# Early-fusion transformer on one core: the last three runs' sums are cut in two, and the first part's order is made with other durations

## Chip, cores and metric

One core of a Trainium2 chip. The metric is device time in microseconds (us) of one execution; lower is better.

The engines named here: PE (TensorE: matrix products and transposes), DVE (VectorE), ACT (ScalarE), POOL (GpSimd) and SP (SyncE, which here only issues DMAs). Each engine works through a queue of its own in the order in which the program was built; ACT and POOL issue DMAs too. An instruction waits in its queue until the semaphores it names have come, and everything behind it waits with it.

## The reference, cut to what matters

Sixteen samples. A tokenizer (a 2x2 convolution and attention over 441 image tokens) and 128 text tokens give 569 rows of 256 numbers per sample. Layer 0 is attention in windows of 64 rows and then a mixture of 8 experts, of which each row takes its best two. Layer 1 is a linear attention by phases and then an LSTM over the 569 rows, whose output goes through running sums:

```python
h = tokenizer(x); h = concatenate([h, txt], axis=1)            # (16, 569, 256)
h = h + window_attention(layernorm(h))                         # layer 0
h = h + top2_of_8_experts(layernorm(h))
h = h + phase_attention(layernorm(h))                          # layer 1
return h + lstm_ffn(layernorm(h))

def lstm_ffn(x):                                               # (b, t, d)
    lstm_out = lstm(x, W_ih, W_hh, b_ih, b_hh)
    logits = lstm_out @ W_lin.T + b_lin                        # (b, t, 2)
    g = argmax(logits, axis=-1)[..., None]                     # 0 or 1
    w = g * lstm_out
    inc = cumsum(w, axis=1)
    prefix = inc - w
    suffix = inc[:, -1:, :] - inc
    return 2.0 * lstm_out + prefix * fw_att + suffix * bw_att
```

`inc[:, -1:, :]` is the total over all 569 rows, and every row of the output needs it (`suffix`). No row can leave before the last step of the LSTM is done and its sum is known.

## The kernel before

**Orders made by a planner.** The class `Order` (L163) takes a number of streams, which are Python generators. A stream yields the engine and the time that its next piece of work is taken to need (`yield "DVE", 0.43`), or an event to wait for, and then issues the instruction. `Order.run` always lets the stream go on whose piece can start first, by its own account of when each engine comes free. `first.fork(...)` starts a further stream at that point. The yielded times thus only decide the order in which instructions stand in each queue; they are no times of the chip. `"64"` behind a time names the tile shape of the products, `DVE+` and `POOL+` name work of DVE and POOL that the planner does not let run at one time.

**First part (about 0 to 962 us of the span; `first`, an `Order`).** Samples go in 8 pairs `p`, each with 9 chunks `c` of 128 rows (`unit(n)` gives pair and chunk of the n-th of 72 units). The streams: `features` (the convolution, DVE and ACT), `projections` and two `tokens` streams (image attention, mostly PE), `norms` (layernorm ahead of the windows, slot `"w"`), four `windows` streams (each has one unit at a time: transposes, q and k products, scores `wS`, maximum `wtop`, the subtraction of the maximum on POOL at L794, exp on ACT, sums, transposes `wpt`, products `wav` and `wob`), `sent_rows` (layernorm ahead of the experts), `routing` (which two experts) and `send` (POOL issues an indirect DMA for each of a chunk's two copies, L927, into the experts' regions `XS`). `norm` (L657) is used by `norms` and `sent_rows`: statistics on DVE (L661, L664), then on POOL add EPS (L668) and power -1/2 (L669), and for the windows a third one, power +1/2, into the last column of `h` (L671); then DVE subtracts and multiplies (L673). The column is read much later, by L784, on DVE.

**Second part (962 to about 3261 us).** The expert tiles, then the phase attention and the LSTM, ordered by another `Order`, `plan`. The LSTM (`steps`) is a chain of 569 steps, one about every 2.5 us where it runs alone: `gates` products (L1832) on PE, `act` (L1853) on ACT, then on DVE `ab`, the cell, its transposition, `th` on ACT, and `X` (L1896) on DVE, which the next step's products read.

**The sums.** `RUNS` cuts the 569 rows into runs of at most 16 rows; the last three have 16, 8 and 1. For each run `sums_of` (a stream `all_sums`) works once the run's steps are done. What leads to the total: the products for the logits (L1116 `fin`, PE), the carry from the run before (L1926, ACT), `w` (L1931, DVE, twice), the running sum `sum` (L1939, DVE scan, twice). Then the run's rows: `y` (L1946 and L1951, DVE, four pieces), transposes `turned` (L1959, PE), and the addition of the rows kept from before into the tile `O` (L1968, DVE). `fin` and `turned` share one PSUM buffer (tag `fin`).

**The end.** `all_rows` (L2017, DVE) spreads the total, `last` (L2025, L2027, PE) turns it, into the same PSUM buffer; `T1` (L2029) is its copy, for all rows, with L2034 a second copy for the run of one row. Then DVE adds it to the rows in `O` in pieces of 2, 4 and 8 units (L2038; a unit is 128 rows x 256 numbers, 128 KB) and SP and ACT in turn issue the stores of each run (L2042), two units each.

The line numbers in the text are those of the kernel before.

Of the kernel before, what the change touches and what calls it, by code (L numbers as in the profile page):

```python
# [10 lines left out]
F32 = mybir.dt.float32  # L11
# [10 lines left out]
E = 8  # L22
# [275 lines left out]
def kernel(ctx: ExitStack, tc: tile.TileContext, a: dict, out: bass.AP):  # L298
# [301 lines left out]
    def tokens(slot):  # L600

        last = NIMG - 384
        for n in range(slot, 7 * NP, 2):
# [4 lines left out]
            for m in range(2):  # L608
                yield "PE", 0.76, "64"
                for s in range(2):  # L610
                    nc.tensor.matmul(
                        sc[64 * s : 64 * s + 64, :NIMG], QT[s][:, m, 64 * c : 64 * c + 64],
                        fTs[2 * p + s][:, m, :], start=(m == 0), stop=(m == 1),
                    )
# [20 lines left out]
            for t in range(4):  # L635
                m = min(128, NIMG - 128 * t)
                yield "PE", 0.44, "64"
                for s in range(2):
                    nc.tensor.matmul(
                        mm[64 * s : 64 * s + 64, :], PT[:m, t, 64 * s : 64 * s + 64],  # L640
                        TV[s][:m, t, :], start=(t == 0), stop=(t == 3),
                    )
# [14 lines left out]
    def norm(h, to, name, slot):  # L657

        st = wk.tile([128, 6], F32, name=f"{name}_st", tag=f"st{slot}", bufs=1)
        yield "DVE", 0.43  # L660
        nc.vector.bn_stats(st, h[:, :D])  # L661
        mv = wk.tile([128, 2], F32, name=f"{name}_mv", tag=f"mv{slot}", bufs=1)
        yield "DVE", 0.18
        nc.vector.bn_aggr(mv, st)  # L664
        rstd = wk.tile([128, 1], F32, name=f"{name}_rstd", tag=f"rstd{slot}", bufs=1)
        yield "POOL", 0.85 if name[0] == "r" else 1.28
        over = mv[:, 1:2]
        nc.gpsimd.tensor_scalar(over, over, EPS, None, ALU.add)  # L668
        nc.gpsimd.tensor_tensor(rstd, over, mhalf[:, :1], ALU.pow)  # L669
        if name[0] == "w":  # L670
            nc.gpsimd.tensor_tensor(h[:, D + E :], over, half, ALU.pow)  # L671
        yield "DVE+", 0.5
        nc.vector.tensor_scalar(to, h[:, :D], mv[:, 0:1], rstd, ALU.subtract, ALU.mult)  # L673
        return rstd

    def norms():
# [10 lines left out]
    def sent_rows(p, c, h, slot):  # L687
# [9 lines left out]
        rstd = yield from norm(h, XN[p][:, c, :D], f"r{p}_{c}", slot)  # L697
        yield "DVE", 0.19
        nc.vector.scalar_tensor_tensor(
# [4 lines left out]
    def half_of_keys(u, kb, qk, rows, engine):  # L704
        for r in rows:
            own = slice(32 * r, 32 * r + 32)
            yield engine, 0.4
            (nc.scalar.copy if engine == "ACT" else nc.vector.tensor_copy)(
                kb[own, :, :, r, :], qk[own, 1].rearrange("p m (w x) -> p m w x", w=2)
            )  # L710
        first.mark(("keys", u, engine))

    def windows(slot):

        kb, vb = KB[slot], VB[slot]
        for n in range(slot, NC * NP, WINDOWS):
# [13 lines left out]
            for m in range(2):  # L730
                for j in range(2):
                    for k in range(2):
                        yield "PE", 0.25
                        nc.tensor.matmul(  # L734
                            qk[:, j, m, :], wqkv[:, k, D * j + 128 * m : D * j + 128 * m + 128],
                            xT[:, k, :], start=(k == 0), stop=(k == 1),
                        )
# [35 lines left out]
            for k in range(2):  # L773
                yield "PE", 0.06, "64"
                for w in range(2):
# [6 lines left out]
            nc.vector.tensor_reduce(top, S, AX.X, ALU.max)  # L782
# [968 lines left out]
    run_of = {(j, u): r for r, (j, u, _) in enumerate(RUNS)}  # L1751
    sums = {}

# [152 lines left out]
    def sums_of(r, j, u, n, X):  # L1906
# [14 lines left out]

        w = ls.tile([128, 2, NB, n + 1], F32, name=f"w{r}", tag="w2", bufs=1)
        yield "ACT", 0.2
# [5 lines left out]
        for k in range(2):  # L1929
# [4 lines left out]
            )  # L1934
        before = ls.tile([128, 2, NB, n + 1], F32, name=f"sum{r}", tag="sum", bufs=2)
        sums[r] = n, before
        for k in range(2):
# [27 lines left out]
        if "O" in tail:  # L1965
            o = tail["O"][:, tail["at"] : tail["at"] + units, :]
        for i in range(units):
# [4 lines left out]
        if "O" not in tail:  # L1972
            nc.sync.dma_start(PD[:, tail["at"] : tail["at"] + units, :], o)
            tail["stored"] += units
        tail["at"] += units

# [54 lines left out]
    for r, (j, u, n) in enumerate(RUNS):  # L2031
        units, t0 = -(-n // STEPS), BLOCKS[j][0] + u
        if n == 1:
            nc.vector.tensor_copy(by_q(T1[:NB]), last[:NB, 1].rearrange("p k (q x) -> p q k x", q=4))  # L2034
            nc.vector.tensor_tensor(O[:NB, at, :], O[:NB, at, :], T1[:NB], ALU.add)
        elif at == done:
# [3 lines left out]
                T1.unsqueeze(1).to_broadcast([128, done - at, D]), ALU.add,  # L2040
            )
        (nc.sync, nc.scalar)[r % 2].dma_start(  # L2042
            by_rows(out, t0, n),
# [124 lines left out]
```

## Time and profile before

| | |
|---|---|
| device time, median of 3 runs | 3315.19 us (3311.05 to 3320.17) |
| device time of the profiled execution | 3305.14 us |
| its span, first to last instruction | 3303.4 us |
| busy: PE / DVE / ACT / POOL | 2989.9 / 2051.8 / 1486.8 / 815.6 us |
| mean granted TensorE clock | 0.975 |
| first part up to the first expert tile's transposes | 0 to 961.95 us |
| last LSTM step's `X` ends | 3260.77 us |
| DMA queues 1 and 10 in the last 48 us | 4.74 and 4.59 MB |

A busy time is the sum of the times of an engine's instructions, so 2989.9 us of PE says that PE is at work in 91% of the span, in the mean over stages that are limited by different things. A row of the view by windows gives the same for one stretch of time: each engine's busy time with its number of instructions, the granted clock of TensorE, the share of time in which the 16 DMA engines were busy, and what they moved. In the timeline a row is an instruction or several merged: start, length, engine, line, operation, output and inputs, shape, how many, and in brackets how long the engine stood idle before it and what ended that.

### The profile page before, as it was taken

Reading aid. Unit: us, or ns where it says so; the run is one execution under the profiler, and the core shown is the slowest. Engines: PE = TensorE matmul, PEld = TensorE weight load, DVE = VectorE, ACT = ScalarE, POOL = GpSimd, SP = SyncE. Lnnn points to the kernel's source line nnn. Section 1 sums busy time; section 2 is a strip of 40 time slices with the busy share of each in tenths; the row PEclk is TensorE's granted clock in tenths of the full one; section 3 lists DMA queues with packets and bytes.
Section 4 is the critical chain, followed back from the end, with each engine's and each line's share of the span. In section 5 each row is a group of like instructions: output and inputs, shape, how many; then the busy total and the mean of one; then the engine's idle time right before and its main releaser. Section 6 shows DMA issues by size and latency. Waiting matters only on the chain.

```text
span 3303.4 us, 133968 instructions
## 1 busy us (share of the span) xinstructions
PE 2989.9 (91%) x57598; PEld 2205.3 (67%) x57598; DVE 2051.8 (62%) x6946; ACT 1486.8 (45%) x5068; POOL 815.6 (25%) x1579
## 2 busy tenths in 40 slices
PE   6999999999849999997899999999999999899884
PEld 3666666666638888885576767677676766666552
DVE  4678777786742222222676777677777777676555
ACT  3544544454412222222554556556665656454442
POOL 1354465545533332322311101010110010000000
PEclk8999999999979999998999999999999999999997
DMA  5111221101177676773433333333333333233323
GB/s 180 58 62 57 74 85 63 52 31 45 41 240 247 242 254 236 250 245 121 125 89 102 89 91 96 99 92 98 92 88 97 89 100 87 74 96 92 101 86 116
DMA packets 268419, 378.43 MB, mean 115 GB/s; under 512 B 133088, under 2 KB 207888, under 8 KB 255152
## 3 DMA queue, kind: packets, MB, share of 16 engines
q1 hardware_dynamic: 242192, 313.73, 30.1%
q0 software_dynamic: 14160, 38.83, 3.1%
q10 hardware_dynamic: 11472, 17.30, 1.8%
q8 instruction: 451, 7.39, 0.9%
q14 instruction: 144, 1.18, 0.1%
HBM read 252.06 MB, written 117.70 MB: 112 GB/s over the span
## 4 chain that ended last, share of the span: by engine, by line
PE 36%; DVE 7%; ACT 6%; DMA 2%; issue 2%; POOL 0%; SPq 0%; ACTq 0%; DVEq 0%; POOLq 0%
PE gates L1832 13%; PE xm_False L1116 6%; PE out_gate L1841 2%; PE v L1116 2%; ACT act L1853 1%; PE ek L1116 1%; PE eq L1116 1%; ACT th L1889 1%; DMA xo<-XOD 1%; PE r_False L1116 1%; DVE ab L1868 1%; PE po_False L1116 1%; DVE cT L1881 1%; PE ds_False L1116 1%; DVE act L1874 1%
## 5 line engine op out<-in xcount | busy, mean ns | idle before, releaser
L1832 PE MATMUL gates<-W_hh,X 128*16 128x96 f32 (+1 forms) x18176 | 490.8, 248 | 63.9 <-DVE X L1896 60.3
L1832 PEld LDWEIGHTS gates<-W_hh,X 128*16 128x16 f32 (+1 forms) x18176 | 378.3, 103 | 252.9 <-DVE X L1896 236.1
L1327 ACT ACTIVATE hT<-hp,w 128x256 f32<-128x256 f32 (+1 forms) x332 | 132.9, 453 | 448.8 <-PE hp L1320 342.0
L1853 ACT ACTIVATE act<-gates 128x96 f32<-128x96 f32 x568 | 142.1, 250 | 412.1 <-PE gates L1832 403.4
L1116 PE MATMUL xm_False<-W_ih,dxT_False 128*32 128x256 f32 x4352 | 294.3, 382 | 0.8 <-ACT dxT_False L1356 0.6
L1868 DVE SCALAR_TENSOR_TENSOR ab<-act 128x64 f32<-128x64 f32 x568 | 127.9, 225 | 255.6 <-ACT act L1853 248.5
L1334 PE MATMUL y<-w,hT 128*128 128x256 f32 x1208 | 276.3, 381 | 6.9 <-ACT hT L1327 6.8
L1340 DVE TENSOR_TENSOR ys<-y,w 128x512 f32<-128x512 f32 (+1 forms) x83 | 53.4, 644 | 358.5 <-PE y L1334 306.6
L1320 PE MATMUL hp<-xt,w 128*128 128x256 f32 (+1 forms) x1328 | 275.2, 360 | 0.0
L1775 PEld LDWEIGHTS <-nil 128*32 128x32 bf16 x4552 | 186.4, 95 | 119.0 <-issue 60.4
L1334 PEld LDWEIGHTS y<-w,hT 128*128 128x128 f32 x1208 | 226.3, 190 | 41.8 <-ACT hT L1327 11.8
L1320 PEld LDWEIGHTS hp<-xt,w 128*128 128x128 f32 x1328 | 232.8, 190 | 28.7 <-ACT hT L1327 0.2
L1261 POOL DMA_INDIRECT YT<-ys,to x151 | 147.3, 975 | 416.8 <-DVE ys L1340 389.6
L1841 PE MATMUL out_gate<-W_hh,X 128*32 128x64 f32 x9088 | 235.5, 220 | 6.1 <-issue 3.2
L1781 ACT COPY gates<-xc 128x96 f32<-128x96 f32 x569 | 138.6, 244 | 140.9 <-PE gates L1775 62.8
L1841 PEld LDWEIGHTS out_gate<-W_hh,X 128*32 128x32 f32 x9088 | 189.2, 111 | 11.0 <-issue 4.0
L1896 DVE SCALAR_TENSOR_TENSOR X<-toT,th 128x32 f32<-128x32 f32 x569 | 109.6, 193 | 129.2 <-ACT th L1889 126.3
L1889 ACT ACTIVATE th<-cT 128x32 f32<-128x32 f32 x569 | 130.4, 229 | 89.5 <-DVE cT L1881 49.0
L927 POOL DMA_INDIRECT XS<-XN,at x144 | 150.3, 1044 | 51.3 <-issue 24.6
L734 PE MATMUL wqk<-wxT,wqkv 128*128 128x128 f32 x1152 | 150.3, 280 | 7.6 <-ACT wxT L728 7.2
L734 PEld LDWEIGHTS wqk<-wxT,wqkv 128*128 128x128 f32 x1152 | 140.0, 192 | 24.1 <-ACT wxT L728 13.5
L1775 PE MATMUL gates<-nil 128*32 128x96 bf16 x2276 | 132.5, 209 | 24.2 <-ACT act L1853 4.5
(383 smaller groups left out, 6493.8 us busy)
## 6 DMA issues: line engine op xcount, KB each, us to landing
w<-in_wpack SPq DMA_DIRECT2D x83, 1154.0 KB
taps<-in_taps SPq DMA_DIRECT2D x16, 1764.0 KB
xc<-XCD SPq DMA_DIRECT2D x71, 384.0 KB
XCD<-xp_False SPq DMA_DIRECT2D x136, 192.0 KB
yg<-YT SPq DMA_DIRECT2D x72, 256.0 KB
xo<-XOD SPq DMA_DIRECT2D x71, 256.0 KB
xs<-XS SPq DMA_DIRECT2D x68, 258.0 KB
HD<-h SPq DMA_DIRECT2D x72, 128.0 KB
```

The lines of the kernel that those rows point to most:

```text
L734: nc.tensor.matmul(qk[:, j, m, :], wqkv[:, k, D * j + 128 * m : D * j + 128 * m + 128], xT[:, k, :], start=(k == 0), stop=(k == 1),)
L927: fill(0, nc.gpsimd.indirect_dma_start(out=XS[0], out_offset=bass.IndirectOffsetOnAxis(ap=at[:, i, c - lo : c - lo + 1], axis=0), in_=XN[p ...
L1116: nc.tensor.matmul(out[own], lhsT[:, own], rhs, start=start, stop=stop)
L1261: keep(nc.gpsimd.indirect_dma_start(out=YT, out_offset=bass.IndirectOffsetOnAxis(ap=to[:, i : i + 1], axis=0), in_=ys[:, i, :], in_offset= ...
L1320: nc.tensor.matmul(hp[:, i, : 128 * n], w1[:, k, hc * 128 : (hc + 1) * 128], xT[:, k, :], start=(k == 0), stop=(k == 1),)
L1334: nc.tensor.matmul(y[:, i, :], hT[:, hc, 128 * i : 128 * i + 128], w2[:, hc, :], start=(hc == 0), stop=(hc == 3),)
L1775: nc.tensor.matmul(g[32 * q : 32 * q + 32, :n], nil[:, :32], nil[:, :n], start=True, stop=last)
L1832: nc.tensor.matmul(GC[32 * q : 32 * q + NB * (1 + half), :96], before[:, kk, NB * (1 - half) :], Whh[:, kk, own : own + 96], start=False, ...
L1841: nc.tensor.matmul(GO[32 * q : 32 * q + 32, :64], before[:, kk, :], Whh[:, kk, own : own + 64], start=False, stop=(kk == 1),)
L1853: nc.scalar.activation(act[:, :96], GC[:, :96], AF.Tanh, scale=0.5), begun.pop((k, t))
L1868: nc.vector.scalar_tensor_tensor(ab, act[:, :64].rearrange("p (g x) -> p g x", g=2), 1.0, act[:, 64:].rearrange("p (g x) -> p g x", g=2), ...
L1889: nc.scalar.activation(th.rearrange("p k x -> p (k x)"), cT, AF.Tanh, scale=0.5)
```

## The change

Three things. First, the planned times of some pieces of the first part are replaced; in the order of the diff they are the tokens' scores (L611) and products with the values (L639), `norm`'s two pieces, the experts' gate in `sent_rows` (L699), the copies of the keys (L708), the q and k products (L734), the gate's columns (L777, L784) and the copies of the values (L790). Second, in `norm` the power +1/2 of the windows leaves the POOL piece and becomes a forked stream of its own, `deviation`, with three buffers for `mv` in place of one. Third, `sums_of` is cut in two: for the last three runs only what leads to the total is done in the stream, with buffers of their own for `w` and `sum`, and the rest, `rows_of_sums`, is kept in a list; at the end it is drawn from the list once the additions of the first 12 units have been issued. The small copy for the run of one row, now `T2`, is made ahead of that.

```diff
             for m in range(2):
-                yield "PE", 0.76, "64"
+                yield "PE", 0.745, "64"
...
-                yield "PE", 0.44, "64"
+                yield "PE", 0.46, "64"
...
-        mv = wk.tile([128, 2], F32, name=f"{name}_mv", tag=f"mv{slot}", bufs=1)
+        mv = wk.tile([128, 2], F32, name=f"{name}_mv", tag=f"mv{slot}", bufs=3 if slot == "w" else 1)
...
-        yield "POOL", 0.85 if name[0] == "r" else 1.28
+        yield "POOL", 0.9
         over = mv[:, 1:2]
         nc.gpsimd.tensor_scalar(over, over, EPS, None, ALU.add)
         nc.gpsimd.tensor_tensor(rstd, over, mhalf[:, :1], ALU.pow)
         if name[0] == "w":
-            nc.gpsimd.tensor_tensor(h[:, D + E :], over, half, ALU.pow)
-        yield "DVE+", 0.5
+            first.fork(deviation(h, over))
+        yield "DVE+", 0.46
         nc.vector.tensor_scalar(to, h[:, :D], mv[:, 0:1], rstd, ALU.subtract, ALU.mult)
         return rstd
+
+    def deviation(h, over):
+        yield "POOL", 0.6
+        nc.gpsimd.tensor_tensor(h[:, D + E :], over, half, ALU.pow)
...
-        yield "DVE", 0.19
+        yield "DVE", 0.25
...
-            yield engine, 0.4
+            yield engine, 0.46 if engine == "ACT" else 0.53
...
-                        yield "PE", 0.25
+                        yield "PE", 0.225
...
-                yield "PE", 0.06, "64"
+                yield "PE", 0.087, "64"
...
-            yield "DVE", 0.2
+            yield "DVE", 0.22
...
-                yield "ACT", 0.4
+                yield "ACT", 0.47
...
-    sums = {}
+    sums, waiting, LATE = {}, [], 3
...
-        w = ls.tile([128, 2, NB, n + 1], F32, name=f"w{r}", tag="w2", bufs=1)
+        late = r >= len(RUNS) - LATE
+        if late:
+            w = op.tile([128, 2, NB, n + 1], F32, name=f"w{r}")
+            before_ = op.tile([128, 2, NB, n + 1], F32, name=f"sum{r}")
+        else:
+            w = ls.tile([128, 2, NB, n + 1], F32, name=f"w{r}", tag="w2", bufs=1)
+            before_ = ls.tile([128, 2, NB, n + 1], F32, name=f"sum{r}", tag="sum", bufs=2)
...
+        at = tail["at"]
+        tail["at"] += units
+        finish = rows_of_sums(r, n, m, units, at, hf, w, before, X)
+        if late:
+            waiting.append(finish)
+        else:
+            yield from finish
+
+    def rows_of_sums(r, n, m, units, at, hf, w, before, X):
         y = ls.tile([128, 2, NB, n], F32, name=f"y{r}", tag="y", bufs=1)
...
-            nc.vector.tensor_copy(by_q(T1[:NB]), last[:NB, 1].rearrange("p k (q x) -> p q k x", q=4))
-            nc.vector.tensor_tensor(O[:NB, at, :], O[:NB, at, :], T1[:NB], ALU.add)
+            nc.vector.tensor_tensor(O[:NB, at, :], O[:NB, at, :], T2[:NB], ALU.add)
...
+        if at >= 8 and waiting:
+            T2 = op.tile([128, D], F32, name="T2")
+            nc.vector.tensor_copy(by_q(T2[:NB]), last[:NB, 1].rearrange("p k (q x) -> p q k x", q=4))
+            for finish in waiting:
+                for _ in finish:
+                    pass
+            waiting.clear()
```

More of the change, by code (lines that the diff above doesn't have):

```diff
@@ L1934, in sums_of @@
             )
-        before = ls.tile([128, 2, NB, n + 1], F32, name=f"sum{r}", tag="sum", bufs=2)
+        before = before_
         sums[r] = n, before
@@ L1965, in sums_of @@
         if "O" in tail:
-            o = tail["O"][:, tail["at"] : tail["at"] + units, :]
+            o = tail["O"][:, at : at + units, :]
         for i in range(units):
@@ L1972, in sums_of @@
         if "O" not in tail:
-            nc.sync.dma_start(PD[:, tail["at"] : tail["at"] + units, :], o)
+            nc.sync.dma_start(PD[:, at : at + units, :], o)
             tail["stored"] += units
-        tail["at"] += units
     def by_rows(v, u, n):
```

## The prediction, made before the changed kernel ran

> **What bounds the kernel now.** I read the page's slices first, then busy time by windows, then the timeline at the two places that the change touches. The chain of waits gives PE 36% of the span, and in the slices PE stands at 9 tenths nearly everywhere; the middle, 962 to 3261 us, is left out here, since in the built order every instruction of it stands where it stood, up to the last seven LSTM steps. So two stretches count, the first part and the end. By windows (columns: stretch, length, then busy time and instructions of PE, PE's weight loads, DVE, ACT and POOL, the granted clock, DMA share, GB/s):
>
> ```profile
> 100.00:200.00 100.00, 96.11 (x870) 66.24 (x865) 76.06 (x202) 49.20 (x132) 33.89 (x64) 1.00 0.15 52
> 300.00:400.00 100.00, 92.80 (x850) 65.05 (x846) 74.57 (x206) 49.29 (x134) 54.42 (x98) 1.00 0.22 77
> 500.00:600.00 100.00, 91.36 (x836) 65.05 (x834) 75.53 (x203) 48.94 (x133) 53.23 (x93) 1.00 0.21 73
> 870.00:962.00 92.00, 41.85 (x361) 32.37 (x362) 56.72 (x210) 22.45 (x59) 46.83 (x83) 0.72 0.41 134
> 3261.00:3273.00 12.00, 3.82 (x40) 1.81 (x40) 8.24 (x26) 0.25 (x1) 0.00 (x0) 0.56 0.01 2
> 3273.00:3301.00 28.00, 0.00 (x0) 0.00 (x0) 18.54 (x12) 0.00 (x0) 0.00 (x0) 0.50 1.00 332
> ```
>
> The reader is to see: until 870 us PE is the bound and idle for 4 to 9 us in a hundred; from 870 to 962 us nothing is full, this is a chain from one engine to the next; then 12 us in which no row leaves, and 28 us in which the DMA engines are full (share 1.00) while DVE is not (18.54 of 28).
>
> The handover of the first part, timeline around its last window unit (unit 8 of the last pair):
>
> ```profile
> 912.75 1.37 POOL L927 DMA_INDIRECT XS<-XN,at  x1 [3.12 <-DVE at L920]
> 913.37 0.68 DVE L782 TENSOR_REDUCE wtop<-wS 128x8 f32<-128x512 f32 x1
> 918.21 0.96 POOL L927 DMA_INDIRECT XS<-XN,at  x1 [0.19 <-DVE rank L873]
> 919.23 1.05 POOL L794 TENSOR_TENSOR wS<-wS,wtop 128x512 f32<-128x512 f32 x1
> 920.31 0.63 ACT L796 ACTIVATE wS<-wS 128x512 f32<-128x512 f32 x1 [4.14 <-POOL wS L794]
> ```
>
> Its maximum is there at 914.05, but five sends stand ahead of the subtraction, which starts 5.2 us late.
>
> The end of the kernel:
>
> ```profile
> 3245.69 0.72 DVE L1939 TENSOR_TENSOR_SCAN sum<-begins,w 128x272 f32<-128x272 f32 x1
> 3247.03 0.23 DVE L1868 SCALAR_TENSOR_TENSOR ab<-act 128x64 f32<-128x64 f32 x1 [0.62 <-ACT act L1853]
> 3260.58 0.19 DVE L1896 SCALAR_TENSOR_TENSOR X<-toT,th 128x32 f32<-128x32 f32 x1 [0.23 <-ACT th L1889]
> 3269.28 0.66 PE L2025 MATMUL last<-ident,all_rows 128*128 128x128 f32 x2 [0.55 <-DVE O L1968]
> 3270.41 0.42 DVE L2029 COPY T<-last 128x256 f32<-128x256 f32 x1 [1.23 <-PE last L2027]
> 3270.87 19.85 DVE L2038 TENSOR_TENSOR O<-O,T 128x512 f32<-128x512 f32 x12
> 3271.71 27.27 SPq L2042 DMA_DIRECT2D out<-O  x19
> ```
>
> From the last `X` (3260.77) to the first addition (3270.87) 10.1 us go by, and the stores can't be hastened once they flow: only an earlier start helps, if DVE then feeds them.
>
> **The end, step by step.** In the built order, DVE's queue after the last `X` holds: `w` twice and scans twice of the run of 8, the same of the run of 1, `all_rows` twice, T1, T2, additions. From rows: 0.70 (two `w`, from 3262.29) + 0.81 (two scans) + 0.08 for two hops = 1.59; the carry on ACT 0.25 and a hop 0.06; two short scans 0.34 and a hop 0.04, 2.28 so far (the short product on PE, 0.42, must wait for the PSUM buffer until `w` has read it; it and the short `w`, 0.38, lie beside the scans). `all_rows` 0.48 from start to end of both, hop 0.04; `last` 1.09 (3269.28 to 3270.37) and hop 0.10; T1 0.42, T2 0.41 and hops: 4.9. Before: 10.1. Gain 5.2.
>
> Two losses ahead of that. The pieces `y` of the run of 16 stood one to a step, in DVE's idle time; now two stand behind one another, after a scan, ahead of `ab`, in two steps. The scan ends at 3246.41 and `ab` started at 3247.03, so 0.62 is free; the pair needs 0.68 + 0.48 and two hops of 0.04, 1.24. Each such step is 0.62 late: 1.24, and everything of the chain waits for it. And half of the run of 8's product stands ahead of the last step's `gates`: half of 0.65, 0.32. Together 1.56.
>
> Then the feed. With the first addition at 0, additions end at 0.68, 1.29, 2.4 and 3.5 (12 units); now follow `O` of the run of 16 (0.75), four `y` of the run of 8 (1.45), the next addition (1.1), `O` 0.42, four `y` 0.75, an addition of 2.2, `O` 0.41, and on. So units 13 to 16 are there at 6.8 and not 4.6, 17 to 24 at 10.2 and not 6.8, 25 to 32 at 12.8. A unit takes the DMAs 28.0 / 71.1 = 0.39, and flow starts 1.45 after the addition (3271.55 to 3273.0). Twelve units last from 2.15 to 6.83; the next come to flow at 8.25 (1.42 dry) and last to 9.81; the next at 11.65 (1.84 dry) and last to 14.8, where the following are there (14.25). Dry: 3.26. PE's transposes for these rows lie beside additions. Dry DMAs are nowhere in the trace of before, so from both sides: 0 if queued stores cover it, 4.8 if DVE also waits for PE in each of the two short runs (some 0.75 each). I take 3.26, which the rows give.
>
> Sum for the end: -5.2 + 1.56 + 3.26 = -0.4 (between -3.6 and +1.2).
>
> The Trainium skill speaks against moving transposes to the end ("TensorE: Matmul & The Clock Gate", section "What's actually happening"): after an idle window of about 3.4 us the array's clock is halved. The trace agrees: clock 1.00 until 3262.5, 0.50 after; the four transposes of the run of 16 took 0.74 at 1.00, the four of `last` 1.09 at 0.50. By the rule the moved ones cost half as much again, and beside additions that is nothing on the path; by the warm row the sum would be the same.
>
> **The first part.** No instruction is added or taken away; all of PE's work is the same, so only idle time can change: from 100 to 870 us the windows of 100 us show 3.9 to 8.6 idle, some 55 between 50 and 870 in all, and 50 from 870 to 962.
>
> (a) PE's queue. For each hand-over inside a unit I took the time the other engines need, from the quiet stretch after 902 us (0.5 from `wtr` to `wqk`, 2.75 to `wsc`, 0.95 to `wv`, 4.5 to `wpt`, 0.75 to `wav`, 0.5 to `wob`; for tokens 1.75 and 1.0), and the PE work that stands between the two in the queue, by mean durations. What is short, summed over the 72 and 56 units: before 16.8 until the last token product and 11.0 after it; changed 15.7 and 7.4. So -1.1 and -3.6.
>
> (b) POOL's queue. Sends standing directly ahead of a window's subtraction: 39 before (twice five, the pair above among them), 21 in the changed order (never more than three). A send is 1.27 from start to start (847.68, 848.95), so 18 x 1.27 = 22.9 less lateness, over four window streams that cover one another, and mostly hidden by PE's full queue. Between 0 and 22.9; nearest is the count in (a), where PE sees little: I take 2 beside it.
>
> (c) `deviation`. The POOL piece ahead of `rstd` never held it (L673 waits for L669, and L671 came after); 0.57 of POOL moves to later, at nothing, since POOL is idle for 45% even from 200 us on. If that cover is gone, L784 waits, see the last rival. The two other `mv` buffers only allow this.
>
> (d) The handover. Unit 8's subtraction now stands ahead of the sends, but `at` of the first four chunks stands behind its `wS` on DVE, so all sends start later against unit 8, and `r_8`, its last norm, stands behind six of them. By the rows the row-sums start some 4.3 after the maximum, not 6.9, and `r_8` gives about 1.2 back. The gain is 1.4 to 5.2; the count in (a) says 3.6, and I take that once, not twice.
>
> Sum of the first part: -1.1 - 2 - 3.6 = -6.7. Another order can fall out either way: eight stretches at the best seen idle (3.9) would be 23 less, at the worst (8.6) 15 more; with stretches scattering by some 2 us, eight of them scatter by about 6. All told -7.1: the profiled execution 3305.14 would go to 3298. It lay 10 under the median of 3315.19, so I set the forecast on the median: 3308.
>
> **Rivals.**
> 1. The better times pay in the whole first part: PE idles 4.5 in a hundred, as in the best two stretches (100 to 200: 3.9), not 6.7: 8.2 x 2.2 = 18, with 3.6 and 0.4 some 22: 3293. For it: 39 against 21 sends. Against it: the count of short hand-overs hardly moves before the last tokens.
> 2. It doesn't do what it says: rows that were to lie beside the stores starve them, as summed, and the first part's order is only another one: -0.4, 3315.
> 3. Slower: the put-off power is late. In 22 of 72 units a send now stands directly ahead of it, 1.27 + 0.57 = 1.84; L784 on DVE needs it, and behind L784 stand other units' maxima and key copies, for which PE waits. Four paid in full (7.1 / 1.84) eat the gain, ten make it slower by over 0.3%; if half of 22 x 1.84 = 40 shows, 3308 + 20 = 3328. For it: DVE's strict order and 76 of 100 us busy. Against it: L784 comes after `wv`, several us after the norm.
>
> **How the numbers follow.** Forecast 0.45, rivals 0.18, 0.23 and 0.14. 0.3%, 10 us, is about what can be told from no change here. The scatter of 6 puts a quarter of the forecast's share under 3305.2; with most of rival 1: faster 0.29. Most of rival 3 is above 3325: slower 0.13. Same 0.58. The range leaves out half of rival 1 and most of 3: 3296 to 3321; the forecast's own is 3300 to 3316.
>
> **What would show it.** First expert transposes at about 955 and not 961.95; last `X` to first addition some 4.9; two steps of 3.1 us near the end; DMA share below 1 between the third and the tenth us of the stores; no five sends ahead of a subtraction. Wrong would be: L784 waiting for POOL (rival 3), idle PE under 5 in a hundred (rival 1), a store flow without a gap (end -3.6).

## The result, and the profile after

The changed kernel took 3303.47 us in the median of 8 runs (3297.12 to 3308.24), beside 3316.76 us for the kernel before on the same chip (8 runs, 3309.78 to 3324.33). The ratio is 0.9959, with a 95% interval of 0.9945 to 0.9972, so 9 to 18 us faster. A second time, in the experiments, it was 0.9975 (0.9963 to 0.9987). The forecast was 3308 us, in the range 3296 to 3321.

The profiled execution after took 3304.34 us with a span of 3302.6 us, where that of before had 3305.14 and 3303.4. These two differ by 0.8 us, because the execution shown of before was quicker than every timed run beside the changed kernel. What each edit does is therefore read stage by stage and from several executions, below. Here and below, "both edits" are the new planned times and the power's own stream.

The line numbers of the changed kernel are higher by 4 in the first part (L794 is now L798, L927 is L931) and by 4 to 24 at the end: `X` L1900, the scan L1949, `y` L1965 and L1970, `all_rows` L2035, `last` L2043 and L2045, T1 L2047, T2 L2061, the additions L2055, the stores L2066.

The view by windows of the changed kernel (stretch, length, busy time and instructions of PE, its weight loads, DVE, ACT and POOL, granted clock, DMA share, GB/s):

```profile
100.00:200.00 100.00, 96.70 (x888) 67.41 (x885) 78.23 (x215) 48.78 (x133) 34.98 (x65) 1.00 0.15 52
300.00:400.00 100.00, 92.41 (x829) 65.45 (x828) 76.40 (x205) 47.87 (x132) 53.51 (x94) 0.98 0.21 74
500.00:600.00 100.00, 92.84 (x804) 68.30 (x802) 75.09 (x208) 48.35 (x133) 54.19 (x97) 0.97 0.22 74
870.00:960.00 90.00, 40.20 (x402) 29.88 (x399) 59.71 (x216) 23.15 (x62) 52.33 (x93) 0.76 0.46 151
3273.00:3276.00 3.00, 1.20 (x4) 0.46 (x4) 3.00 (x8) 0.00 (x0) 0.00 (x0) 0.50 0.84 244
3276.00:3279.00 3.00, 0.00 (x0) 0.00 (x0) 3.00 (x3) 0.00 (x0) 0.00 (x0) 0.50 0.56 170
```

In the first three of these stretches PE's idle time is close to what it was: 3.3, 7.6 and 7.2 us in a hundred, against 3.9, 7.2 and 8.6. The granted clock is 0.98 and 0.97 in two of them, and was 1.00; what that costs is told under the table of stages. At the end the DMA engines have gaps (0.84, then 0.56) that they didn't have before, just in the time in which DVE is busy without a pause (3.00 of 3.00).

The timeline of the changed kernel at the handover of the first part, at the same unit 8 as before (start, length, engine, line, operation; in brackets the idle time ahead and what ended it):

```profile
909.23 0.68 DVE L786 TENSOR_REDUCE wtop<-wS 128x8 f32<-128x512 f32 x1
911.77 1.04 POOL L798 TENSOR_TENSOR wS<-wS,wtop 128x512 f32<-128x512 f32 x1
916.00 1.09 POOL L931 DMA_INDIRECT XS<-XN,at  x1 [3.19 <-DVE LG L703]
```

The maximum is there at 909.91 and the subtraction starts 1.9 us later, not 5.2; the sends come behind it.

And at the end:

```profile
3247.57 0.72 DVE L1949 TENSOR_TENSOR_SCAN sum<-begins,w 128x272 f32<-128x272 f32 x1
3248.32 0.67 DVE L1965 SCALAR_TENSOR_TENSOR y<-sum,weights,X 128x256 f32<-128x256 f32 x1
3249.03 0.48 DVE L1970 SCALAR_TENSOR_TENSOR y<-w,weights,y 128x256 f32<-128x256 f32 x1
3249.43 0.22 DVE L1872 SCALAR_TENSOR_TENSOR ab<-act 128x64 f32<-128x64 f32 x1
...
3263.83 0.19 DVE L1900 SCALAR_TENSOR_TENSOR X<-toT,th 128x32 f32<-128x32 f32 x1 [0.23 <-ACT th L1893]
3266.32 0.41 PE L2043 MATMUL last<-ident,all_rows 128*128 128x128 f32 x2 [1.22 <-DVE all_rows L2035]
3266.99 0.42 DVE L2047 COPY T<-last 128x256 f32<-128x256 f32 x1 [0.68 <-PE last L2045]
3267.66 3.54 DVE L2055 TENSOR_TENSOR O<-O,T 128x512 f32<-128x512 f32 x4
```

A scan and two `y` now stand ahead of `ab` in one LSTM step: `ab` starts at 3249.43, 0.80 us after `act` began (3248.63); before the change it was 0.28 (3246.75 to 3247.03). From the last `X` (ends 3264.02) to the first addition it is 3.64 us, not 10.1.

### The profile page after: what moved, and what is told of

It reads as the page before. It is cut to its first block, busy times and chain, and to the rows that moved or that the text cites. A ratio compares the mean times of both kernels' runs of the same rounds, so it can differ in the third digit from the quotient of the medians.

```text
span 3302.6 us, 133922 instructions
## 1 busy us (share of the span) xinstructions
PE 2990.7 (91%) x57598; PEld 2212.4 (67%) x57598; DVE 2045.1 (62%) x6946; ACT 1490.5 (45%) x5068; POOL 817.4 (25%) x1579
## 4 chain that ended last, share of the span: by engine, by line
PE 36%; DVE 7%; ACT 6%; issue 2%; DMA 1%; POOL 0%; SPq 0%; ACTq 0%; DVEq 0%; POOLq 0%
PE gates L1836 13%; PE xm_False L1120 6%; PE out_gate L1845 2%; PE v L1120 2%; ACT act L1857 1%; ACT th L1893 1%; PE ek L1120 1%; PE eq L1120 1%; PE po_False L1120 1%; DVE ab L1872 1%; PE r_False L1120 1%; DVE cT L1885 1%; DVE act L1878 1%; DVE X L1900 1%; PE ds_False L1120 1%
## 5 line engine op out<-in xcount | busy, mean ns | idle before, releaser
L1338 PEld LDWEIGHTS y<-w,hT 128*128 128x128 f32 x1208 | 226.3, 190 | 41.2 <-ACT hT L1331 11.2
L1900 DVE SCALAR_TENSOR_TENSOR X<-toT,th 128x32 f32<-128x32 f32 x569 | 109.9, 193 | 130.0 <-ACT th L1893 125.6
L931 POOL DMA_INDIRECT XS<-XN,at x144 | 149.9, 1041 | 60.8 <-issue 25.3
L1386 POOL TENSOR_SCALAR d_False_rstd<-d_False_mv 128x2 f32<-128x2 f32 (+1 forms) x36 | 8.9, 249 | 585.9 <-DVE d_False_mv L1378 333.8
```

The costliest lines, as they stand in the source:

```text
L931: fill(0, nc.gpsimd.indirect_dma_start(out=XS[0], out_offset=bass.IndirectOffsetOnAxis(ap=at[:, i, c - lo : c - lo + 1], axis=0), in_=XN[p ...
L1338: nc.tensor.matmul(y[:, i, :], hT[:, hc, 128 * i : 128 * i + 128], w2[:, hc, :], start=(hc == 0), stop=(hc == 3),)
```

## The stages, from thirteen profiled executions

Each row is one profiled execution, its times read from the timeline. The columns: where the last token product ends; from there to the end of the last routing product (`pos`, the end of the chain of the first part); from there to the first expert transposes; when these start; the middle, from there to the end of the last `X`, less the lengthening of the last steps where the sums are cut; and from the last `X` to the end of the span. The lengthening itself is in the last column. The kernels after the second are the experiments.

| kernel | tokens end | to last `pos` | to first expert | first expert | middle | last `X` to end | steps longer |
|---|---|---|---|---|---|---|---|
| before | 869.9 | 66.5 | 25.6 | 962.0 | 2298.8 | 42.6 | 0 |
| after | 873.0 | 59.2 | 27.4 | 959.6 | 2303.1 | 38.6 | 1.35 |
| before_again | 875.9 | 68.2 | 24.9 | 968.9 | 2304.7 | 42.6 | 0 |
| tail_only | 874.6 | 66.3 | 25.0 | 965.9 | 2310.3 | 38.9 | 1.35 |
| first_only | 874.6 | 59.6 | 28.4 | 962.6 | 2313.2 | 42.5 | 0 |
| rows_at_40 | 874.3 | 59.9 | 28.1 | 962.3 | 2305.5 | 37.1 | 1.35 |
| after_again | 873.5 | 59.7 | 27.9 | 961.1 | 2302.1 | 39.1 | 1.3 |
| costs_only | 884.9 | 70.8 | 25.3 | 980.9 | 2298.4 | 42.2 | 0 |
| dev_only | 888.0 | 56.5 | 27.9 | 972.4 | 2298.7 | 42.6 | 0 |
| loads_late | 875.5 | 59.7 | 26.2 | 961.5 | 2305.3 | 38.8 | 1.3 |
| rows_40_y_in_steps | 871.8 | 59.4 | 28.0 | 959.1 | 2298.4 | 36.4 | 0 |
| fork_and_sums | 889.3 | 56.6 | 27.3 | 973.2 | 2299.1 | 36.2 | 0 |
| y_in_steps_again | 875.2 | 59.5 | 27.8 | 962.6 | 2302.8 | 36.5 | 0 |

wih_late, a fourteenth, is told where it belongs. The table can be read down its columns. The end repeats within 0.5 us for one order, the chain from the last tokens to the last `pos` within 2, the first part as a whole within 7. The middle, in which PE and DVE have the same order in all these kernels (but for the memsets of loads_late), scatters by 15 us (2298.4 to 2313.2). That is more than any part of this change is worth. A single pair of profiles, like the two above, can't show a gain of 10 us; their stages can. Part of the scatter goes with the granted clock: the mean of the whole execution is 0.971 to 0.973 in the three with the longest middle (first_only, wih_late, tail_only) and 0.975 to 0.978 in four of the five with the shortest. The fifth, costs_only, has 0.972, but its clock was low in the first part (0.95, below). Why the clock differs was not found.

The clock also shows what became of the first part up to the last token product. From 50 us to there PE is idle for 55.2 to 59.2 us in the three executions with the order of before (57.8 in the mean), and for 54.1 to 55.2 us in the eight with both edits (54.9, wih_late among them). But the clock was at half for 0.6 to 3.4 us before, and for 20.5 to 23.9 us with both edits, in pieces of 3.41 or 6.83 us, most of them at the same places in each execution. PE's busy time rose from 765.6 to 769.1 us, by about as much as the idle time fell. One such place, before and after:

```profile
200.00:250.00 50.00, 45.48 (x385) 32.97 (x383) 39.32 (x108) 27.16 (x75) 38.49 (x68) 1.00 0.26 90
```

```profile
200.00:250.00 50.00, 45.58 (x413) 33.61 (x413) 36.70 (x96) 25.05 (x65) 38.01 (x65) 0.93 0.17 60
```

## The experiments

Ratios are to the kernel before, run beside each experiment on the same chip: its medians were 3315.47 us (28 runs) beside the first four, 3316.32 (31 and 17) beside the next seven, and 3314.42 (13) beside the last. A ratio differs from the quotient of the two medians by up to 0.0008; gains given in us are by the ratio, so for costs_only 13 us where the medians differ by 11.

### The kernel before, once more

No edit.

> The kernel before, a second profile, since its first profiled execution (3305.14 us) was quicker than all eight timed ones (3309.78 to 3324.33). Theory A (what the change gains sits in the first part and at the end, and the middle, whose instructions stand in the same order, only scatters): first expert transposes again at 961 to 963 us, last X to the end of the span again 42.6 +- 0.5, and the middle between them longer than the 2298.8 us of the first profile, some 2305 to 2312. Theory B (the change shortens the middle too): the middle is 2299 again and the whole 3305.

3317.97 us in one run. The first part is 7.0 us longer than in the profile shown, the middle 5.9 (2304.7), the end the same to 0.04. So the middle does scatter, but the expectation's 961 to 963 us for the first part was wrong: that scatters too. Setting the forecast on the median, and not on the profiled execution, was right by this.

### One half of the change at a time

tail_only has the cut sums alone, first_only the planned times and the power's stream alone.

```diff
--- tail_only: against before, only
+        late = r >= len(RUNS) - LATE
...
+        if late:
+            waiting.append(finish)
+        else:
+            yield from finish
...
--- first_only: against before, only
+        yield "POOL", 0.9
...
+            first.fork(deviation(h, over))
+        yield "DVE+", 0.46
...
```

> Only the sums divided, the first part as before. Theory A: handover at 962, last seven steps 1.35 longer, last X to the end 38.6 instead of 42.6, so 2.7 us less than before: ratio 0.9992. Rival (the end carries most of the 13 us): ratio 0.997 or less.

> Only the first part's planned times and the forked power, the end as before. Theory A: handover at 959.6 instead of 962, last X to the end 42.6, so 2.3 us less: ratio 0.9993. Rival (the first part's order carries most of the 13 us, by what it does to the middle or by more than one profile shows): ratio 0.997 or less.

tail_only: 3312.87 us, ratio 0.9991 (0.998 to 1.0003), some 3 us. first_only: 3310.62 us, 0.9982 (0.997 to 0.9994), some 6 us. Together 9, and after_again gave 0.9975, which is 8. Each of these is uncertain by 4 us, and tail_only's interval includes no gain at all; within that the halves add, and neither alone is a story for the whole. The profile of tail_only shows its part more sharply: the end is 3.7 us shorter and the last steps 1.35 longer.

### Rows drawn later

```diff
-        if at >= 8 and waiting:
+        if at >= 40 and waiting:
```

> The changed kernel, but the rows of the last three runs are drawn after the additions of 48 units and not of 12. Theory A (rows drawn early starve the stores): DMA share 1.0 from the first store to the last, last X to the end some 3 us shorter than in the changed kernel, 35.5 instead of 38.6; ratio to before about 0.001 lower than the changed kernel's. Rival (the gap in the stores is made up by faster flow after it): 38.6 as it is.

3304.39 us, ratio 0.9964 (0.9952 to 0.9977). In the time that can't be told from the changed kernel; in the profile the additions take 33.0 us from the first to the end of the span, not 34.9 and not the 32.5 of before. So the late rows beside the stores cost 2.4 us, and drawing them after 40 units takes back 1.9 of it. The DMA share stays at 1.01 or above from the first full window on.

### The changed kernel once more

> The changed kernel once more, beside the three that follow. What the two halves gave apart (0.9982 for the first part, 0.9991 for the sums) multiplies to 0.9973, and the two whole versions gave 0.9959 and 0.9964. If the halves simply add, this run falls at 0.997; if something of the two helps the other, at 0.996. The stages should repeat: last token product to last routing product 59.2 to 59.9 us, last routing product to first expert transposes 27.4 to 28.4, last X to first addition 3.6 or 4.1 us by whether the last two transposes meet the full clock, last X to the end 38.6 to 38.9.

3305.97 us, 0.9975 (0.9963 to 0.9987). The stages repeat as expected, but for the last, 39.1. That is what the halves give if they simply add (0.9973); the first comparison's 0.9959 was nearer to the rival, and the two together don't decide.

### The two edits of the first part, each alone

costs_only and dev_only were built with the sums of before. Their expectations say the sums were the changed ones; that is a slip, and their ratios are read against first_only's 0.9982. costs_only's also names 0.63 for `DVE+`; it was built with 0.46, and with 1.5 for the POOL piece that still holds both powers. In dev_only the power is planned with 0.6 in its own stream, and the piece that it leaves with 0.85 in place of 1.28.

```diff
--- costs_only: against before, only the planned times
-        yield "POOL", 0.85 if name[0] == "r" else 1.28
+        yield "POOL", 0.9 if name[0] == "r" else 1.5
...
-        yield "DVE+", 0.5
+        yield "DVE+", 0.46
...
--- dev_only: against before, only the stream (and mv's buffers)
...
-        yield "POOL", 0.85 if name[0] == "r" else 1.28
+        yield "POOL", 0.85
...
-            nc.gpsimd.tensor_tensor(h[:, D + E :], over, half, ALU.pow)
+            first.fork(deviation(h, over))
...
```

> The new planned times (DVE+ 0.63 and the power's 0.9) without the power put in a stream of its own; the sums as in the changed kernel. Counted from the built order as for the prediction, PE's queue is short of 13.4 us at the end of the first part, against 11.0 before and 7.4 with both edits. If the count holds, the stretch from the last token product to the last routing product is 66 to 69 us and the gain of the first part is gone (ratio near 0.9991, that of the sums alone). Rival: the better planned times carry the gain by themselves, and the stretch is 59 to 61 us as with both.

> The power put in a stream of its own, with the planned times of before (DVE+ 0.5, the power's 0.85); the sums as in the changed kernel. By the same count PE is short of 7.7 us at the end of the first part, nearly as little as with both edits (7.4). If the count holds, the stretch from the last token product to the last routing product is 59 to 62 us, and the ratio is that of the changed kernel within 0.0007. Rival: without the better times the order of the sends and the subtractions stays as before (36 sends directly ahead of a subtraction against 39) and the stretch stays at 66 to 68 us.

costs_only: 3326.89 us, ratio 1.0040 (1.0026 to 1.0055): 13 us slower than before, by the measured durations alone. dev_only: 3310.15 us, 0.9986 (0.9976 to 0.9997), by the time as fast as both edits. Where costs_only loses is in the view by windows, costs_only first, then the kernel before:

```profile
200.00:300.00 100.00, 85.27 (x730) 60.16 (x728) 70.03 (x184) 43.58 (x120) 48.79 (x85) 0.95 0.20 69
```

```profile
200.00:300.00 100.00, 93.61 (x890) 69.31 (x889) 79.87 (x206) 50.98 (x140) 55.31 (x95) 1.00 0.21 72
```

In this stretch every engine does less than before, so none of them is the bound there: PE is idle for 14.7 us rather than 6.4, and the granted clock of what it does do is 0.95. PE's longest single waits there are 3.5 us for `tQ` and 2.5 for a norm. From 500 to 600 us it is the same, PE idle for 12.4 us at a clock of 0.95. Which of the planned times makes this order worse was not tried.

The planner's order was thus not better for knowing better times. The count used in the prediction, of hand-overs for which PE's queue is short, can be held against the table. At the end of the first part 7.4, 7.7, 11.0 and 13.4 us counted went with 59.5, 56.5, 67.0 and 70.8 us measured: the orders with the stream are told from those without, and those without from each other, but not 7.4 from 7.7; a counted us was worth some two. For the long stretch before that the count says nothing of the time: 16.8 before and 15.7 with both edits went with the last token product at 873.4 and 873.9, while either edit alone put it at 884.9 and 888.0. The count of sends ahead of a subtraction ranks nothing either: by their traces costs_only has 25 and is the slowest, the kernel before 39, and dev_only 31 (its expectation says 36).

### The stream alone, with the best sums

```diff
--- against rows_40_y_in_steps (below), only
-        yield "DVE+", 0.46
+        yield "DVE+", 0.5
...
```

and so for the other planned times: all are those of before.

> The sums as in rows_40_y_in_steps, and of the first part only the power in a stream of its own, with all planned times as before the change. dev_only and costs_only were built with the sums of before, not with the changed ones as their expectations say, so they are read against the first part's edits together (0.9982): the power apart gave 0.9986, the better times by themselves 1.0040. If the power in its own stream is what the first part gains by, this run's ratio is within 0.0007 of that of rows_40_y_in_steps beside it. If dev_only's profile (last token product at 888.0 us against 873 to 876, first expert transposes at 972.4 against 960 to 969) shows an order that is slower, and its time was luck, this run repeats these two times and is 8 us slower than rows_40_y_in_steps.

3306.83 us, 0.9971 (0.9961 to 0.998), beside 0.9966 (0.9952 to 0.998): within 0.0007. And its profile repeats that of dev_only, the token products' end at 889.3 us (888.0) and the first expert at 973.2 (972.4). Neither reading of the expectation is whole. By the profiles the first part of this order is 7 us longer than that of before and 12 longer than with both edits; by the times it is some 3 to 5 us better than before. Its middle was 2298.7 and 2299.1, at the short end of the scatter, and that of costs_only, the other kernel with a late first part, 2298.4. Whether a first part with more idle PE is given back in the middle, or two executions fell so by chance, stays open.

### Where the handover gives back

In all the profiles with both edits the chain to the last `pos` is 7.5 us shorter (59.5 against 67.0 in the mean), but the first expert transposes come only 4.6 us earlier (961.0 against 965.6). Between the two 2.8 us are given back (27.9 us against 25.1, without the two experiments below). The SP queue, before and after:

```profile
932.89 0.45 SPq L1043 DMA_DIRECT2D W_hh<-in_W_hh  x1
951.06 0.87 SPq L1241 DMA_DIRECT2D w<-in_wpack  x2
952.53 5.32 SPq L1249 DMA_DIRECT2D xs<-XS  x3
...
965.70 0.47 SPq L1044 DMA_DIRECT2D W_ih<-in_W_ih  x1
```

```profile
927.78 0.43 SPq L1047 DMA_DIRECT2D W_hh<-in_W_hh  x1
928.26 0.80 SPq L1048 DMA_DIRECT2D W_ih<-in_W_ih  x1
948.91 0.94 SPq L1245 DMA_DIRECT2D w<-in_wpack  x2
952.26 3.42 SPq L1253 DMA_DIRECT2D xs<-XS  x3
```

`W_ih`, 1 MB for the last stage, has slipped ahead of the first experts' loads, and the DMA share is 0.99 to 1.08 from 930 to 945 us, where the zero rows and the last rows are sent too. The diff doesn't touch these loads: their place on SP's queue came out of the build with the new order of the rest. The first load of `xs`, the rows for the first expert, is issued 20.0 us after the last `pos`, not 16.1, and in the changed kernel it also waits for the zero rows, which in the kernel before it doesn't (the view of SP's waits, from 925 to 970 us; in all, times, longest):

```profile
SPq L1253 <- DMA XS<-zeros: 1.8, 1, 1.8
```

In the same time VectorE's planning of the tiles, the same instructions, has pauses:

```profile
937.10 0.19 DVE L1183 TENSOR_REDUCE first<-past 128x4 f32<-128x32 f32 x1 [1.19 <-DVE past L1180]
938.53 0.17 DVE L1185 TENSOR_SCALAR first<-first 128x4 f32<-128x4 f32 x1 [1.05 <-DVE first L1184]
```

and takes 15.9 us, from the last `pos` to the last `where`, not 11.0. Full DMA engines alone don't make these pauses. In the kernel before the plan runs from 936.4 to 947.6 us without one of over 0.3 us, as it does in before_again, tail_only and costs_only, while the DMA engines are as full:

```profile
940.00:945.00 5.00, 0.00 (x0) 0.00 (x0) 4.57 (x17) 0.77 (x4) 3.36 (x6) 0.50 1.07 346
```

All ten executions of kernels with the power's own stream have pauses, the two without the new times the fewest (one and two; their plan takes 12.5 and 12.8 us to its very end, that of the kernel before 11.2). Two experiments put loads back by a dependency, a memset of one column of each target after the third tile: loads_late does so for all of the last stage's loads, wih_late for W_ih.

```diff
--- loads_late
-        yield "at", ("tile", 0, 1)
+        yield "at", ("tile", 0, 3)
...
+        for t in (lin[:, :, :1], lstm_b[:, :1], lb[:, :1], Whh[:, :, :1], Wih[:, :, :1], ...):
+            yield "DVE", 0.1
+            nc.vector.memset(t, 0.0)
--- wih_late
+        yield "at", ("tile", 0, 3)
+        yield "DVE", 0.1
+        nc.vector.memset(Wih[:, :, :1], 0.0)
         nc.sync.dma_start(Wih, kxn("W_ih"))
```

> The changed kernel with the loads of the last stage's weights (3.0 MB of them stand ahead of the first experts' loads, W_ih's 1.0 MB among them, which stood behind those before the change) put behind the first nine tiles' loads, by a small memset of each target after the third tile. Theory: the 2.8 us that the changed kernel gives back between the last routing product and the first expert transposes (27.4 to 28.4 us against 24.9 to 25.6) are these loads, which now come 1.0 MB more and fill the DMA engines while the zero rows, the last rows and the first expert weights are sent and the tiles are planned. Then that stretch falls to 20 to 25 us, VectorE's plan of the tiles from 15.7 to about 11 us without its gaps of 0.5 to 1.2 us, PE stays over 0.98 busy from the first tile on, and the time falls by 3 to 7 us below the changed kernel's. Rival: the gaps come from GpSimd's last sends, which now run beside the plan; then the plan still takes 15 to 16 us, and the stretch stays above 26 us.

> The changed kernel with W_ih's load alone (1.0 MB; Wk's 0.25 MB comes ahead in its place) put behind the first tiles' loads, for the part of the 2.8 us given back that goes to it. All 3.0 MB put back took the stretch from the last routing product to the first expert transposes from 27.4 to 28.4 us down to 26.2 and the plan of the tiles from 14.3 to 15.9 us down to 13.4, which left some of it open. If W_ih is what moved, this run has the same 26 us, or 25 as before the change; if the weights count for little, and the rest is GpSimd's sends, which end 8.4 to 9.3 us after the last routing product rather than 7.2, the stretch stays at 27 to 28 us.

The stretch fell to 26.2 us in loads_late and 26.6 in wih_late (last `pos` 932.56, first expert 959.14), from 27.9 in the mean of the six without such an edit (27.4 to 28.4). So by one execution each the loads are 1.3 to 1.7 of the 2.8 us, most of that by W_ih, and the expected 20 to 25 us were wrong. What is left: with no weights at all in the way the DMA engines are just as full, as the windows of loads_late show,

```profile
940.00:945.00 5.00, 0.00 (x0) 0.00 (x0) 4.07 (x12) 1.99 (x5) 4.08 (x8) 0.50 1.09 257
```

with zero rows (2.0 MB in all) and the last rows, at 257 GB/s; and POOL's last send ends 9.3 us after the last `pos` (944.54), in the changed kernel 8.4, before 7.2. In loads_late SP's load of the first expert weights waits for these sends (9.5 us at once) and is issued 16.4 us after the last `pos`, before 14.7, and its `xs` load at 17.9 no longer waits for the zero rows. So what is left fits the later sends, but they were not tried alone. VectorE's plan takes 16.6 us in wih_late, the longest of all, and 13.4 in loads_late. Its length doesn't set the end of the stretch, since wih_late has a short one. In the time nothing was won: loads_late 3308.14 us, 0.9979 (0.9969 to 0.9989), wih_late 3311.74 in one run.

### The best of it

```diff
--- rows_40_y_in_steps: against the changed kernel
+            if n > STEPS:
+                for _ in range(4):
+                    yield next(finish)
+                next(finish)
             waiting.append(finish)
...
-        if at >= 8 and waiting:
+        if at >= 40 and waiting:
```

The four `y` of the run of 16 stay in the stream, one to a step, as before the change; only what follows them is put off.

> The changed kernel with the rows drawn at the 40th unit rather than the eighth, and with the four pieces of `y` of the run of 16 left in the stream, one to an LSTM step, instead of put off. Expected: the two steps of 3.01 us and the last one of 2.83 fall back towards 2.50 (up to 1.3 us less), the stores run on without the gaps that cost 2.4 us (rows_at_40 took back 1.9 of them), last X to the end 37.1 us, and the time is 2.5 to 3 us below the changed kernel's: a ratio 0.0008 to 0.0009 lower than it would have beside it, 0.995 to 0.9966. Rival: the four pieces are not hidden in the steps they now stand in either, and lengthen these by 0.3 to 0.6 us each; then only the 1.5 to 1.9 us of the rows are won.

> rows_40_y_in_steps once more. In its profile no LSTM step is longer than 2.51 us and last X to the end is 36.4 us, against 38.6 us and 1.35 us of longer steps in the changed kernel: 3.6 us less, a tenth of a per cent. The changed kernel had 0.9959 and 0.9975. If these 3.6 us are real and nothing takes them back, this run's ratio is near 0.9956 and its profile has the same 36.2 to 36.5 us with every step at 2.50; if the first run's 0.9966 is all there is, the version is as fast as the changed kernel.

3305.18 us, 0.9966 (0.9952 to 0.998), and 3300.68 us, 0.9958 (0.9943 to 0.9973). The end of the second run, timeline and windows:

```profile
3262.72 0.19 DVE L1900 SCALAR_TENSOR_TENSOR X<-toT,th 128x32 f32<-128x32 f32 x1 [0.23 <-ACT th L1893]
3262.83 0.48 DVE L1974 SCALAR_TENSOR_TENSOR y<-w,weights,y 128x256 f32<-128x256 f32 x1
...
3265.22 0.19 DVE L1900 SCALAR_TENSOR_TENSOR X<-toT,th 128x32 f32<-128x32 f32 x1 [0.23 <-ACT th L1893]
...
3269.06 13.49 DVE L2059 TENSOR_TENSOR O<-O,T 128x512 f32<-128x512 f32 x9
```

```profile
3276.00:3279.00 3.00, 0.00 (x0) 0.00 (x0) 3.00 (x2) 0.00 (x0) 0.00 (x0) 0.50 1.03 347
```

A `y` alone fits into the time in which DVE waits for `act` (0.86 us of it stay idle in the last step), so each step is 2.50 us again, the last one too. The additions run on without a pause, nine pieces in 13.49 us, and the DMA engines stay full. The end is 6.1 to 6.4 us shorter than before in three executions (with fork_and_sums), where the changed kernel's is 2.2 to 2.7 net. In the time two runs of each have 0.9966 and 0.9958 against 0.9959 and 0.9975: the 3.6 us agree with that and are too small to be shown by it.

## Why the prediction was right, point by point

- **Lead path, 10.1 to 4.9.** Right, and 0.8 to 1.3 us too cautious: 3.64 or 4.1. Pieces that were added up lie partly over each other: the two `w` and scans took 1.24 us from the last `X`, not 1.59, T1 and T2 0.74 together, not 0.83. And `last`, set at 1.09 as before, took 0.63 in all where the clock had not fallen yet.
- **Two steps 0.62 longer each, the last 0.32.** Measured 0.50, 0.51 and 0.33: 1.35 for 1.56. The mechanism was the stated one, and rows_40_y_in_steps took it away.
- **Stores run dry for 3.26.** Measured 2.4, in the windows foreseen.
- **The end in all, -0.4.** The three terms were off in the same direction by 1.3, 0.2 and 0.9, and gave -2.7 (-4.05 from last `X` to the end, +1.35). tail_only's 3 us agree.
- **(a) and (b), the long stretch, -1.1 and -2.** Nothing in the time: the last token product ends at 873.4 us in the mean of three executions with the order of before, and at 873.9 in eight with the new one, wih_late (873.36) among them. Rival 1 falls with this. The step that failed is "all of PE's work is the same, so only idle time can change": PE's idle time fell by 3.0 us, near the 3.1 forecast, but its busy time rose by 3.4, with the clock at half for some 20 us more. That the clock makes this rise is argued from these numbers, not tried. The near hit of the idle time may be luck, since it scatters by 4 us in the order of before.
- **(a) and (d), the handover, -3.6.** The chain to the last `pos` gained 7.5, twice the count; 2.8 were given back behind it, which the prediction didn't look at, since SP's queue wasn't compared. Net -4.6. The forecast for the whole first part, -6.7, is more than this and than the 6 us of first_only's time, but within the interval of the latter (2 to 10).
- **(c), the put-off power at nothing.** Right, and rival 3 falls: in the changed kernel L788, the reader of that column, waited 8.8 us in all, 19 times, for `wv` on PE and never for POOL. The row is from the view of that line, under "its engine sat idle before it until":

```profile
  PE wv L781: 8.8, 19
```

- **What would show it.** First expert transposes at 955: 959.1 to 962.6, so this sign failed. Otherwise the signs came: no sends ahead of unit 8's subtraction, steps of 3.01 us, dry DMA engines.

So the total, -7.1, was near the 8 of the second comparison by luck in part: an end taken 2.3 us too low and a handover 1 too low stood against a long stretch taken 3.1 too high. The stages account for some 7 us. The 13 of the first comparison are more than that, and the difference stays open; its interval begins at 9. By the prediction's own mark of 0.3% the first comparison is "faster", to which it had given 0.29, and the second is not.

The prediction also cites an idle window of about 3.4 us ahead of the halved clock. The halving is there, at 3262.5 us. An empty window isn't: in the kernel before PE's last product ahead of it ran from 3261.59 to 3262.23, and its longest pause in the steps ahead was 1.5 us.

## What to carry to other kernels

An order made by a planner isn't priced edit by edit: the measured durations alone lost 13 us, the power in its own stream alone won 5, and both together won 6; build the order, try it, and keep what was measured. Where work is only reordered, look at the granted clock beside the idle time: the busy time need not stay. When work is put off behind a store stream, keep the pieces that fit in waits where they were, and put the others behind so many additions that the stores have a stock. After a change to one queue's order, look through the queues that nobody ordered (here SP's) for a load that has slipped ahead.

## What the runs showed of the hardware that had not been expected

- The four transposes of `last` come 3.2 to 3.5 us after the run of 8's logit product, with one short product (0.32 us) in between, in every kernel with the cut sums. In five profiles they ran at the full clock (0.41 us for two and 0.38 for two), in four at half (0.66 and 0.63); the changed kernel and rows_40_y_in_steps, each profiled twice, had one of each. The granted clock fell 2.4 to 4.9 us after that logit product. The Trainium skill ("TensorE: Matmul & The Clock Gate", section "What's actually happening") says that the window by which the clock is halved runs freely, whatever the kernel does, so that the point varies from run to run. The nine profiles agree; it is 0.46 us of the end.
- In the eight executions with both edits the granted clock was halved five or six times between 50 us and the last token product, for 3.41 or 6.83 us each. In the 3.4 us ahead of each of these PE was at work for 0.5 to 1.9 us, not idle throughout. What share of work keeps the clock was not measured.
- DMA engines that are full by count (share 1.09) moved 257 GB/s of zero rows and scattered rows, and 398 GB/s of expert weights (955 to 960 us in the same run).
- VectorE's short dependent instructions paused, mostly for 0.5 to 1.2 us at a time, in the plan of the tiles of ten executions, and in none of four others with the same instructions and equally full DMA engines (share 1.04 to 1.06 over the plan). The ten have the power's own stream, and their last sends run later beside the plan. What holds the instructions was not found.
